# Four short moves in a four-layer graph network: exponentials, a kept product, column sums and copies change their places in the engines' queues

## The chip, the cores and the metric

The kernel runs on one core of a Trainium2 chip. The core has a matrix engine (TensorE, PE in the profile; its weight loads are PEld), VectorE (DVE), ScalarE (ACT), GpSimd (POOL) and SyncE (SP), which here issues the transfers. Each engine works through its own queue in order; an instruction that needs another engine's result waits on a semaphore, and everything behind it in that queue waits too. The metric is device microseconds for one execution; the median over several runs counts. The profile comes from one profiled execution.

## The reference

Input x is 128 batches of 64 nodes with 256 features. Four layers follow each other, each of the form `x = layernorm(x + layer(x))`.

- Layer 0: attention over the graph. `Wh = x W`; scores `leaky_relu(s1[i] + s2[j])`, masked by the adjacency; `softmax(e) Wh`. The softmax is what the change touches.
- Layer 1: attention over 512 edges with four heads, `leaky_relu(Q[src] + K[dst])` against a vector per head, softmax per source node, weighted values, and an output product.
- Layer 2: `A_hat` times x, a product 256 to 512, a batch norm, relu, a product 512 to 256, and a batch norm.
- Layer 3: two graph products (called gcn below), and then for p = 1, 2, 3, 4 an LSTM over windows of p neighbouring nodes; the last hidden state replaces the last node of each window.

```
for p in range(1, MAX_SKIP + 1):
    wins = h[:, :nw * p, :].reshape(Bv * nw, p, Hd)
    last = _lstm_last(Wih[p - 1], Whh[p - 1], bih[p - 1], bhh[p - 1], wins)
    h = h.at[:, idx, :].set(last.reshape(Bv, nw, Hd))
```

## The kernel before

**Layers 0 and 1 (0 to 460 us)** run together. The 8192 rows are cut into 16 chunks (index q) of 512 rows. A main loop over q issues eight steps of layer 1's edge work for chunk q (`l1_graph`: product z in one of two z banks, L357, then ScalarE's relu into u, L359, which sets the bank free). Between these steps the list `between` places pieces of layer 0 for chunks q + 1 and q + 2 and pieces of layer 1's end for an older chunk (`v_a`, `v_b`, `v_c`). `step` makes the scheduler keep each piece's instructions behind the last TensorE instruction of the step before. Layer 0's softmax of a chunk is in `l0_c`: transposed scores, mask, row maximum mx (L271), four exponentials with row sums (L274), and the reciprocal ri (L277). `l0_d` then transposes the exponentials (L283). `l1_qv` makes queries and values of the next chunk: queries m (L320), values m (L323), spad (L332), qs (L330, L331) and, as the last ScalarE instruction of the piece, the values' copy v (L333). L428 reads v on TensorE; L463 and L467 belong to layer 1's sums.

**Layer 2 (524 to 765 us)** computes its 2x2 blocks of products with seven multiplications in place of eight (class `Seven`). `multiply` (L827) fills a bank, `use` (L837 to L855) drains it: product 1 and product 5 are kept (L837; L841 with the bias, on ScalarE), product 3 goes out at L843 or L846, product 6 and 7 are added to kept product 1 on VectorE (L839, L852), and GpSimd adds kept 6 or 7 with 5 into the result (L847, L853). The kept tiles are `kept[0..3]` and one more place in the room of a weight (wq): products 1 alternates between two places by the job's parity, products 5, 6 and 7 have one each. The statistics for the batch norm (L933) go into st1 and st2.

**Layer 3 (765 to 2043 us)** works on four pairs of groups of 16 batches, one `lstm` generator for each pair. Within a pair p = 1 comes first: for groups n = 0, 1 the gates g, i, o as seven products of 512 columns (class `Wide`, TensorE at L1445). These need column sums of the hidden rows, four GpSimd subtractions per group (`column_sums`, L1399 to L1402), written to wx. Then p = 2, 3, 4, with class `Gate` (TensorE at L1708). A gate's products are kept or added on ScalarE (L1723) and VectorE (L1725 to L1736), with GpSimd's two adds in product 7 (L1731, L1732). ScalarE applies the gate's function (L1741), VectorE the products of the cell and the output (L1621, L1622, L1599, L1608), GpSimd the product for gate f (L1618); hidden sums hs follow at L1572 to L1577. The order within each engine is written out by hand: `given` holds each instruction behind the one issued before it on its engine. Helpers record many operations on the line L116.

The `lstm` generator yields at numbered points (units). The table `side` says which other parts advance there: the next pair's gcn with its norm (x2r, L1300; L95, L96, L85, L98, L86, L100), the next weights (`prepare`), and `final` for finished blocks. A block is one of four positions s of a group g. `final` lets GpSimd copy the block out of H into hd (L1843, two copies), turns it (VectorE's stream transpose L1244 into st, a store to way and loads back on SP), adds it to the saved input x3r (L1858), and normalizes and stores it. For the blocks s = 0 to 2 it runs at units u and u + 2, with u = 34 + 4 s + 2 n. The last position reads its values from the tile the LSTM wrote, without copies; the very last two blocks of the kernel are issued after the loop (L1863, L1864).

## Time and profile before

| what | value |
|---|---|
| median of 3 runs | 2041.83 us (2041.1 to 2047.78) |
| the profiled execution | 2044.78 us |
| its span, first to last instruction | 2043.0 us |
| granted TensorE clock, mean | 0.988 |
| TensorE busy | 1938.6 us |
| VectorE busy | 1252.3 us |
| ScalarE busy | 987.1 us |
| GpSimd busy | 878.0 us |

By stage, TensorE is busy 368.8 of the 390 us of layers 0 and 1 behind their start, 231.8 of 241 in layer 2, 353.2 of 365 in pair 0, 305.2 and 305.5 of 310 in pairs 1 and 2, 258.2 of 266 in pair 3, and 13.8 of 27 in the tail.

How to read it: lines of waits give an engine, the line that waited, what it waited for, and then the time in total, the number of times and the longest. Lines of the timeline give the start and the duration in us, the engine, the line, the operation, the tile it writes, the tiles it reads and their shapes, and in brackets the idle time before it and what ended that. Idle time costs something only where the engine that sets the end stands still.

### The profile page before, as it was taken

The page shows a single profiled execution, that of the slowest core. Times are in us where ns is not written, and L with a number is a line of the kernel's source. Part 1 is how long each engine was busy: PE and PEld are TensorE (multiplying, and loading weights), DVE is VectorE, ACT ScalarE, POOL GpSimd, SP SyncE. Part 2 cuts the span into 40 slices and gives each one's busy share as a digit, 9 for nine tenths or more (in the row PEclk, how much of TensorE's full clock was granted, in tenths as well). Part 3 has the DMA queues.
Part 4 walks back from the last instruction along what each step waited for, and adds up shares of the span by engine and source line. Part 5 has one row for each costly group of instructions (what it writes and reads, how often), then busy time and mean ns, then how long its engine had stood idle before and what let it go on. Part 6 is the DMA issues. An engine that isn't in the chain of part 4 may idle for free.

```text
span 2043.0 us, 31508 instructions
## 1 busy us (share of the span) xinstructions
PE 1938.6 (95%) x11447; PEld 1335.4 (65%) x11447; DVE 1252.3 (61%) x2763; ACT 987.1 (48%) x1892; POOL 878.0 (43%) x1017
## 2 busy tenths in 40 slices
PE   5989999998999989899999999999999999999997
PEld 4667777675554446577668477677577667578685
DVE  7465665564456555765566775566865557664566
ACT  2766667766345623644333644343544333543333
POOL 1123333343345543564545544445543435444264
PEclk9999999999899999999999999999999999999999
DMA  6353343332202134432332233132143032131022
GB/s 155 61 73 60 79 79 49 61 56 41 49 22 49 42 123 151 175 125 94 119 140 83 93 130 134 42 130 91 56 152 117 19 114 69 41 119 78 0 64 71
DMA packets 236540, 173.84 MB, mean 85 GB/s; under 512 B 150625, under 2 KB 213601, under 8 KB 233057
## 3 DMA queue, kind: packets, MB, share of 16 engines
q1 hardware_dynamic: 234528, 169.86, 29.3%
q8 instruction: 90, 1.47, 0.3%
q0 software_dynamic: 1024, 1.05, 0.2%
q10 hardware_dynamic: 832, 0.92, 0.1%
q14 instruction: 66, 0.53, 0.1%
HBM read 110.18 MB, written 61.60 MB: 84 GB/s over the span
## 4 chain that ended last, share of the span: by engine, by line
PE 69%; DVE 15%; ACT 5%; POOL 4%; issue 3%; DMA 2%; SPq 1%; DVEq 0%; POOLq 0%; ACTq 0%
PE l L1708 25%; PE l L1664 7%; PE l L1445 4%; PE pz L827 4%; PE pz L756 3%; PE m L253 2%; PE e L348 2%; PE m L320 2%; PE m L442 2%; PE g L1344 2%; PE pz L1025 2%; PE z L357 2%; PE m L323 2%; DVE cell L1622 1%; PE g L1332 1%
## 5 line engine op out<-in xcount | busy, mean ns | idle before, releaser
L1708 PE MATMUL l<-xs,wx 128*128 128x256 f32 (+1 forms) x896 | 277.2, 400 | 5.7 <-DVE gate L1727 3.9
L1708 PE MATMUL l<-hs,wh 128*128 128x256 f32 (+1 forms) x896 | 276.2, 400 | 3.6 <-DVE hs L1572 3.1
L1723 ACT ACTIVATE kept<-l 128x256 f32<-128x256 f32 (+1 forms) x224 | 88.6, 402 | 332.7 <-PE l L1708 331.3
L86 POOL TENSOR_TENSOR ln_rs<-ln_rs,mhalf 128x2 f32<-128x2 f32 (+2 forms) x98 | 86.2, 880 | 358.3 <-DVE ln_rs L98 352.7
L1708 PE MATMUL l<-H,wx 128*128 128x256 f32 (+1 forms) x672 | 210.7, 402 | 4.3 <-DVE gate L1736 3.4
L1708 PE MATMUL l<-hid,wh 128*128 128x256 f32 (+1 forms) x672 | 208.9, 400 | 0.0
L1708 PEld LDWEIGHTS l<-xs,wx 128*128 128x128 f32 x896 | 169.0, 190 | 50.2 <-issue 5.5
L1708 PEld LDWEIGHTS l<-hs,wh 128*128 128x128 f32 x896 | 169.5, 190 | 46.7 <-DVE hs L1572 5.7
L1741 ACT ACTIVATE gate<-gate,bias 128x512 f32<-128x512 f32 (+1 forms) x280 | 170.6, 657 | 42.0 <-DVE gate L1732 34.8
L1664 PE MATMUL l<-H,wx 128*128 128x256 f32 (+5 forms) x672 | 185.2, 432 | 4.9 <-DVE H L116 2.7
L359 ACT ACTIVATE u<-z 128x1024 f32<-128x1024 f32 x128 | 130.3, 1025 | 68.1 <-PE z L357 67.3
L1664 PEld LDWEIGHTS l<-H,wx 128*128 128x128 f32 x672 | 119.0, 190 | 65.3 <-issue 34.1
L1708 PEld LDWEIGHTS l<-H,wx 128*128 128x128 f32 x672 | 125.9, 190 | 42.4 <-DVE gate L1736 7.4
L1708 PEld LDWEIGHTS l<-hid,wh 128*128 128x128 f32 x672 | 127.5, 190 | 31.7 <-issue 2.9
L1731 POOL TENSOR_TENSOR gate<-gate,kept 128x256 f32<-128x256 f32 (+1 forms) x84 | 65.1, 775 | 153.9 <-DVE kept L1729 153.6
L331 DVE TENSOR_TENSOR qs<-m,qs 64x256 fp32r<-64x256 f32 x128 | 53.9, 422 | 105.0 <-ACT qs L330 103.2
L357 PE MATMUL z<-gath_r,qs 128*128 128x512 f32 x256 | 100.2, 479 | 0.7 <-ACT u L359 0.4
L1630 ACT ACTIVATE gate<-cell 128x512 f32<-128x512 f32 (+1 forms) x88 | 58.6, 666 | 85.9 <-DVE cell L1622 63.8
L1576 POOL TENSOR_TENSOR hs<-hid 128x256 f32<-128x256 f32 (+1 forms) x28 | 26.0, 928 | 168.3 <-DVE hid L1608 85.1
L1736 DVE TENSOR_TENSOR gate<-l,gate 128x256 f32<-128x256 f32 (+1 forms) x112 | 50.0, 446 | 61.8 <-POOL gate L1731 37.5
L1618 POOL TENSOR_TENSOR cell<-gate,cell 128x512 f32<-128x512 f32 (+1 forms) x56 | 75.5, 1369 | 28.4 <-ACT gate L1741 28.4
L1725 DVE TENSOR_TENSOR gate<-l,kept 128x256 f32<-128x256 f32 (+1 forms) x112 | 49.1, 439 | 57.1 <-ACT gate L1741 33.0
(375 smaller groups left out, 4090.1 us busy)
## 6 DMA issues: line engine op xcount, KB each, us to landing
wx<-sums SPq DMA_DIRECT2D x9, 2048.0 KB
wh<-sums SPq DMA_DIRECT2D x9, 1792.0 KB
way<-st SPq DMA_DIRECT2D x54, 256.0 KB
st<-way SPq DMA_DIRECT2D x216, 64.0 KB
xin<-in_x SPq DMA_DIRECT2D x16, 512.0 KB
ld<-table SPq DMA_DIRECT2D x16, 512.0 KB
x_dram<-y SPq DMA_DIRECT2D x16, 512.0 KB
x2r<-x_dram SPq DMA_DIRECT2D x32, 256.0 KB
```

Of the source, the lines that this page charges most:

```text
L86: nc.gpsimd.tensor_tensor(dst, dst, mhalf[:, :n], OP.pow)
L357: nc.tensor.matmul(z[:, k, :], L1[q]["qs"][c][:, s, k * P:(k + 1) * P], gath_r, start=True, stop=True)
L359: nc.scalar.activation(u, z, AF.Relu)
L756: nc.tensor.matmul(p_, w1[:, k, m * P:(m + 1) * P], Aq(q)[:, k * QT:(k + 1) * QT], start=k == 0, stop=k == KD - 1)
L827: nc.tensor.matmul(self.bank[at], lhs, rhs, start=first and n == 0, stop=n == len(self.terms) - 1, skip_group_check=True)
L1445: nc.tensor.matmul(self.bank[at], lhs, rhs, start=new, stop=True, skip_group_check=True)
L1618: nc.gpsimd.tensor_tensor(c, t, c, OP.mult)
L1664: nc.tensor.matmul(b, w.raw[0][:, k, at, m, :], x, start=k == 0, stop=k == KD - 1)
L1708: nc.tensor.matmul(self.banks[j], lhs, rhs, start=src == 0, stop=src == 1)
L1723: nc.scalar.activation(self.keep(j), b, AF.Copy)
L1731: e.tensor_tensor(t[0][:, 1], t[0][:, 1], k[5], OP.add)
L1741: given(lambda: nc.scalar.activation(dst, dst, f, bias=b))
```

## The change

It has four parts.

- Layer 0. The four exponentials and the reciprocal become a piece of their own, `l0_x`. In the main loop it is held behind the last ScalarE instruction issued before it (`behind`), which is the values' copy of `l1_qv(q + 1, 0)`, in iterations in which layer 1's own softmax is due (S not negative). In the others it follows `l0_c` as before.
- Layer 2. Kept product 5 alternates between two tiles by the job's parity, kept product 7 has the place in wq. The memory for one more tile comes from st2, which now lies in two pieces in the tiles mask and spads[0].
- Layer 3, p = 1. In pairs 1 to 3 the second group's column sums are issued right behind the first group's, ahead of all gates, and no longer ahead of the first group's gate o. The gcn block with the norms moves from unit 0 (twice) to units 2 and 4 of the pairs 1 and 2.
- Layer 3, `final`. The generator has a further `yield` behind the two copies and is advanced at u - 1, u, u + 2; so the copies are issued one unit before the turn. The yield is in the branch of the blocks 0 to 2.

What the scheduled program shows of it: TensorE's order is the same but for one swap of a values' matmul (L323) with two of L320 in iteration q = 2. On ScalarE the four exponentials move in six places, in the iterations q = 2, 4, ..., 12, from ahead of spad, qs and v to behind v: two of them, a spad, the other two, and then u. On GpSimd the copies L1843 now stand ahead of the add L1731 of gate f (they stood behind it, ahead of L1618), and for the other group ahead of the L1731 of gate i. On SP the block's store to way goes ahead of the first load of x3r. The norms of pairs 1 and 2 go from before the pair's first adds on VectorE to behind the add of product 7, in gate o for the first group and in the second group's gate g for the second.

```diff
@@ l0_c
             mx = small.tile([P, PQ], F32, name="mx")
             nc.vector.tensor_reduce(mx, e, AX.X, OP.max, negate=True)
+            L0[q]["mx"] = mx
+
+        def l0_x(q):
+            e, mx = L0[q]["e"], L0[q]["mx"]
             sm = small.tile([P, PQ], F32, name="sm")
             for c in range(PQ):
                 nc.scalar.activation(e[:, c, :], e[:, c, :], AF.Exp, bias=mx[:, c:c + 1],
...
+        def behind(do, q):
+            if q < NQ:
+                with tc.issue_after([t for t in nc.cur_bb.bb.instructions
+                                     if t.engine == mybir.EngineType.Activation][-1]):
+                    do(q)
+
...
-                [(l1_t, q + 1), (l1_weights, S), (l0_c, q + 2)],
-                [(sums, q), (l1_qv, q + 1, 0)],
+                [(l1_t, q + 1), (l1_weights, S), (l0_c, q + 2)] + [(l0_x, q + 2)] * (S < 0),
+                [(sums, q), (l1_qv, q + 1, 0)] + [(lambda n: behind(l0_x, n), q + 2)] * (S >= 0),
...
-        st2 = wb.tile([P, M2, NQ, 6], F32, name="st2")
+        st2_rooms = [t[:, :NQ * 6].rearrange("p (q s) -> p q s", s=6) for t in (mask, spads[0])]
+
+        class st2:
+
+            def __class_getitem__(cls, at):
+                return st2_rooms[at[1]][(at[0],) + at[2:]]
...
-        kept = [wb.tile([P, QT], F32, name=f"kept{n}") for n in range(4)] + [flat(wq)]
+        kept = [wb.tile([P, QT], F32, name=f"kept{n}") for n in range(5)] + [flat(wq)]
...
-                self.place = {1: kept[n], 6: kept[2], 5: kept[3], 7: kept[4]}
+                self.place = {1: kept[n], 6: kept[2], 5: kept[3 + n], 7: kept[5]}
...
             if n == 0:
                 given(column_sums, 0)
+                if pair:
+                    given(column_sums, 1)
                 yield "begin", 0
             gates = {}
             for name in "gio":
-                if (n, name) == (0, "o"):
+                if (n, name) == (0, "o") and not pair:
                     given(column_sums, 1)
...
@@ final, behind the copies
+            yield
+
...
-                put(k, final(g, s), u, u + 2)
+                put(k, final(g, s), u - 1, u, u + 2)
...
-                    put(k, block, 0, 0)
+                    put(k, block, 2, 4)
```

More of the change, by code (lines that the diff above doesn't have):

```diff
@@ L566 @@
         l0_c(0)
+        l0_x(0)
         l0_a(1)
@@ L574 @@
         l0_c(1)
+        l0_x(1)
         setup_signs()
```

## The prediction

> **What bounds the kernel now.** I read the busy shares first, then the chain that ended last:

> ```profile
> PE 1938.6 (95%) x11447; PEld 1335.4 (65%) x11447; DVE 1252.3 (61%) x2763; ACT 987.1 (48%) x1892; POOL 878.0 (43%) x1017
> ...
> PE 69%; DVE 15%; ACT 5%; POOL 4%; issue 3%; DMA 2%; SPq 1%; DVEq 0%; POOLq 0%; ACTq 0%
> ```

> TensorE is busy 1938.6 of 2043.0 us. The change leaves the matmuls as they are (one pair of small ones swaps places), so it can work only on the 104.4 us in which TensorE stands still. Its own waits come next (us in total, times, longest):

> ```profile
> PE m L428 <- ACT v L333: 9.5, 6, 2.3
> ...
> PE l L1445 <- DVE gate L116: 4.7, 5, 1.1
> ...
> PE l L1708 <- DVE gate L1727: 3.9, 5, 1.0
> ...
> PE l L1708 <- DVE gate L1736: 3.4, 8, 0.4
> PE g L1231 <- DVE st L1229: 3.3, 1, 3.3
> PE m L253 <- issue: 3.1, 1, 3.1
> PE l L1708 <- DVE hs L1572: 3.1, 3, 1.1
> ```

> Each row but L1231 and L253 belongs to a place that the change touches; one more, `PE pz L827 <- ACT kept L841`, is 2.6 us, once. Behind three of the rows stands a wait of VectorE: L1244, the transpose of a finished block, waits for GpSimd's copies at L1843, 41.8 us in 20 waits.

> [...] L1843's copies last 399 ns by the median row and two in a row take 0.74 us, so both readings agree within 10%. [...] under GpSimd's sums two such VectorE adds took 3.17 us, and two multiplies 2.24, where an undisturbed one takes 0.69.

> **A: layer 0's exponentials** (six places; five have a copy of values to gain by). In the timeline ScalarE makes four exponentials (184.53 to 186.17), then spad, qs, and then:

> ```profile
> 186.78 0.60 ACT L333 ACTIVATE v<-m 128x512 f32<-128x512 f32 x1
> 187.28 1.02 ACT L359 ACTIVATE u<-z 128x1024 f32<-128x1024 f32 x1
> ```

> and TensorE, in its timeline:

> ```profile
> 187.43 1.16 PE L428 MATMUL m<-am,v 64*64 64x64 f32 x62 [1.45 <-ACT v L333]
> 188.52 0.73 PE L357 MATMUL z<-gath_r,qs 128*128 128x512 f32 x2
> ```

> With the exponentials behind it, v is ready near 185.0 and the 1.45 us are gone. But TensorE's next work, the z of L357, needs one of two z banks, which the u at 187.28 to 188.29 sets free. ScalarE has no idle time from 184.53 on, and the same instructions (four exponentials of about 0.39, their accumulator reads, spad, qs, v) still stand ahead of that u. It ends at 188.3 to 188.4 again, z starts at 188.45 in place of 188.52: the stall moves one step on, to "z waits for u". Gain 0.07 x 5, say 0.3 in all. Above: if u came in time, 1.45 x 5 = 7.2. Below: the e transposes (L283) and the reciprocal come later; if they came late by 0.2 in each place, +1.0.

> **B: two places for kept product 5, another for 7.** ScalarE's L841 (617.27) waited for GpSimd's L853 (615.98 to 617.24), the last reader of the one place, and TensorE lost 2.55 us at product 3. With two places L841 is done near 613.9. Product 7 then waits for VectorE:

> ```profile
> 617.27 0.69 DVE L933 BATCH_NORM_STATS2 st<-Z 128x6 f32<-128x512 f32 x1 [1.75 <-POOL Z L853]
> 617.88 0.67 DVE L839 TENSOR_TENSOR kept<-pz,kept 128x512 f32<-128x512 f32 x1
> ```

> L839 frees product 7's bank and stands behind statistics that wait for the same L853. It ends at 618.56 as before, against product 7's old start at 618.98: gain about 0.36, between 0 and 2.55. The statistics' rooms in mask and spads[0] add no instruction: 0.

> **C: second group's column sums behind the first's; norms later** (pairs 1 to 3; norms in pairs 1 and 2). Today GpSimd makes the second group's four sums at 1141.42 to 1147.40, and VectorE's SBUF operations queue with them:

> ```profile
> 1146.31 2.24 DVE L116 TENSOR_TENSOR wh<-wh,hs 128x512 f32<-128x512 f32 x2 [0.19 <-ACT wh L116]
> 1148.47 0.68 DVE L116 TENSOR_TENSOR gate<-l,wh 128x512 f32<-128x512 f32 x1
> ```

> TensorE's product 4 waits for that add: 1.12 us at 1148.08, 1459.80 and 1770.96. In the same pair's second group, where no sums run, the multiplies take 0.69 each. Pair 3 has no norms and the same gap, so it is the sums. Moved, they run at about 1132.5 to 1138.5 and end before GpSimd's next duty at 1140.19. The add is there by 1147.2: -1.12 x 3 = -3.4. Against it: in pairs 1 and 2 each norm is 1.95 us of VectorE (L1300 0.69, L95 2x0.37, aggregates 0.30, two small ones 0.22) and 2.3 us of GpSimd (L86, two L100), now ahead of adds that free banks: hid<-l,wh (1150.25, after 1.10 us idle) and cell<-l,wh (1155.34, followed by 0.86 idle), which TensorE needs at about 1157.2 and which would be there at 1157.0 to 1157.8. I take 0.6 per pair back, bounds 0 and 1.15: C = -3.4 + 1.2 = -2.2. The norm's stores on SP move from 1138 to 1158; SP's next load waits for TensorE until 1166.4 and the reader is due at 1174: hidden, with 15 us to spare.

> **D: the finished blocks' copies one unit earlier** (L1843, 24 places of two copies). What they hold up, in pair 0, step 2:

> ```profile
> 1091.28 0.71 DVE L1244 STREAM_TRANSPOSE st<-hd 128x512 f32<-128x512 f32 x1 [0.94 <-POOL hd L1843]
> ...
> 1097.60 0.42 DVE L1727 TENSOR_TENSOR gate<-l,kept 128x256 f32<-128x256 f32 x1
> ```

> From L1244 to L1727 VectorE has no idle time, and TensorE waits 1.02 for L1727 at 1097.15, then 0.43 for L1736. The copies leave GpSimd's queue behind L1731/L1732 (ended 1090.57, copies to 1091.25) and go in front of L1731, where GpSimd is idle 2.77 us. L1244 then starts at 1090.26, 1.02 earlier, and so does all behind it: about 1.0 per pair at step 2, and 0.43 at step 1 (L1244 waits 0.47 there, TensorE 0.43 at 1069.24). 1.43 x 3 pairs = 4.3. Pair 3 has no other filler: TensorE's gaps of 0.49 (1961.33) and 0.79 (1988.94) follow L1244's waits of 3.27 us, and the other final's wait of 0.47 comes twice: 0.49 + 0.79 + 0.94 = 2.2. At its step 3 VectorE waits 0.88 for the block's load; the block's store can leave 1.1 earlier, but ScalarE's L1741 limits the gain to about 0.5. D = -4.3 - 2.7 = -7.0. On SP the block's store (way) now goes out ahead of the first load of x3r, not behind it; both come a unit before their readers, so nothing on the path. Cover of the moved copies: GpSimd's idle time in front of gate f's L1731, 1.09 to 3.24 us, for 0.75 us of copies; the copies queue ahead of L1731, L1732 and then L1618, and VectorE's L1736 and ScalarE wait for those.

> **Sum.** -0.3 - 0.4 - 2.2 - 7.0 = -9.9 us: the profiled execution, 2044.78 with 1.78 outside its span, goes to 2034.9. It stood 2.95 above the median of the runs, 2041.83; with the same difference the median goes to **2032**.

> **Rivals.** (1) *Stalls come back elsewhere.* B gives nothing, C gives back 1.15 per pair (-1.1), and D gains only where VectorE itself was late, about half, -3.5: together -4.6, 2037.2. For it: so many rows with 0.4 us, each with a next wait close behind. Against: L1244's wait is followed by VectorE work without a hole. (2) *All named gaps close.* A -7.2, B -2.55, C -3.4, D -7.1: 2021.6. Against it, the two z banks and L839. (3) *Slower: the copies hold up gate f.* Undisturbed they take 0.75, under VectorE's two-input operations 0.86 each (the longest seen is 867 ns), 1.7 in all, against GpSimd's idle 1.09 in the tightest places. Where they are over 1.1 us, L1731 and after it L1736 and TensorE are late by about 0.6; in all 24 places that is 14.4, and with A to C's -2.9 the time is 2053. It decides from about 1.1 us per two copies in most places; the median of 399 ns speaks against it.

> **How the numbers follow.** My forecast 0.62, its own range 2028 to 2036.5 (C 1.1 and D 2 to either side); rival 1 0.18; rival 2 0.10; rival 3 0.10. 0.3% of the time, 6.1 us, is about what a measurement of this kernel can tell from no change: faster means under 2035.7. That holds for 0.55 of my 0.62, 0.05 of rival 1's 0.18 and all of rival 2: 0.70. Within it: 0.07 + 0.13 = 0.20. Slower: 0.10. The range 2025 to 2040.5 leaves out rival 3 (0.10), most of rival 2 (0.08) and the edge of rival 1 (0.02).

> **What would show it.** A: L428's wait for v shrinks from 9.5 to about 2.3 (the sixth place is untouched), and "z L357 waits for u L359" grows from 0.4 to about 7. B: the wait of L827 for L841 is gone and one of about 2.2 for L839 is there. C: no 1.12 at L1445 in pairs 1 to 3; VectorE's two-input operations there back at 0.69 each. D: L1244's wait for L1843 falls from 41.8 to under 10, and L1708's rows for L1725, L1727, L1736 and L1572 together from 11.7 to about 5. I would be wrong if L1736 waits longer for L1731 than its 37.5 us now, if z meets its bank in time, or if L1445 waits for the moved adds by over 1.1 per pair.

## The result, and the profile after

The changed kernel took 2038.37 us (median, 2034.17 to 2044.66) against 2044.08 for the kernel before in the same comparison: ratio 0.9974, 95% interval 0.9965 to 0.9983, that is 5.3 us faster (3.5 to 7.2). Forecast was a gain of 9.9 us, to 2032. The time lies outside the forecast's own range (2028 to 2036.5) and inside the wide one (2025 to 2040.5); the gain is little more than half. Measured once more on another occasion, on the chip with the number 0, it was 0.9955 (0.9941 to 0.9968), 9.2 us faster. Most of the experiments below are about what lies between these two results. The profiled execution took 2039.12 us, 5.66 less than the one before.

The page of the changed kernel, busy shares and chain:

```profile
PE 1940.1 (95%) x11447; PEld 1337.8 (66%) x11447; DVE 1248.0 (61%) x2763; ACT 988.0 (48%) x1892; POOL 880.0 (43%) x1017
...
PE 73%; DVE 14%; ACT 5%; DMA 3%; issue 3%; POOL 2%; SPq 1%; DVEq 0%; POOLq 0%; ACTq 0%
```

TensorE's idle time fell from 104.4 to 97.2 us, 7.2 us, but it was busy 1.5 us longer for the same matmuls. TensorE's waits of the changed kernel (line numbers are 4 to 22 higher than before: L357 is L361, L428 is L432, L839 is L857, L1244 is L1262, L1727 is L1747, L1736 is L1756, L1858 is L1880):

```profile
PE z L361 <- ACT u L363: 8.9, 6, 1.8
...
PE l L1728 <- DVE gate L1756: 3.4, 8, 0.4
...
PE l L1728 <- DVE hs L1592: 3.1, 3, 1.2
...
PE l L1728 <- DVE gate L1747: 2.7, 4, 1.1
...
PE pz L845 <- DVE kept L857: 2.3, 1, 2.3
...
PE l L1463 <- DVE gate L116: 1.3, 2, 0.8
```

The first and fifth rows are A's and B's stalls in their new places: the 7.2 us at v became waits of z for u, and the 2.55 us at kept product 5 became 2.30 us at product 7, both as forecast. The last row is down from 4.7: C's three gaps are closed. The rows for L1756 and L1592 did not move at all, and L1747 fell only from 3.9 to 2.7: here is D's shortfall. L1244's wait for the copies has left the list of VectorE's waits; two others have come or grown:

```profile
DVE gate L1756 <- POOL gate L1751: 64.3, 42, 3.4
...
DVE x3r L1880 <- DMA st<-way: 2.7, 3, 1.1
```

The first was 37.5 us. It grew by 27 where 41.8 went, but TensorE's row for L1756 is unchanged, so this wait costs nothing. The second was 0.9 us, once, and its growth costs (see D).

The windows view of the changed kernel shows what no line of the waits does. Columns: stretch, its length, busy time of PE, PEld, DVE, ACT and POOL with counts, then the granted clock, the DMA share and GB/s:

```profile
248.00:250.00 2.00, 1.17 (x81) 1.03 (x72) 0.45 (x2) 1.95 (x10) 0.05 (x1) 1.00 0.47 72
250.00:252.00 2.00, 1.04 (x6) 0.80 (x6) 0.07 (x1) 2.00 (x3) 0.90 (x1) 1.00 0.12 28
252.00:254.00 2.00, 1.78 (x6) 1.34 (x5) 0.00 (x0) 2.00 (x4) 0.96 (x1) 0.56 0.00 0
254.00:256.00 2.00, 2.00 (x7) 1.61 (x6) 0.46 (x2) 1.13 (x4) 0.24 (x1) 0.58 0.06 16
```

At 249.17 TensorE waits 1.79 us for u, one of A's moved stalls; shortly behind it the granted clock is one half, from 252.26 to 255.67, for 3.41 us, and the matmuls take about twice as long: four of L324 fill 1.89 us from 252.37 on, and the next four, which begin behind the stretch, at 255.83, fill 0.87. (The expectations below say 3.3 us.) Busy time weighted with one minus the clock, summed over each microsecond of such a stretch, gives 1.6 to 1.7 us lost each time. Over the whole profile it is 16.6 us before and 22.2 after. Of these 5.6 us, 3.5 lie in the first 60 us, where the stretches at half clock fell differently in the two executions: 10.2 us in all before, 17.1 after. Two stretches behind A's stalls add 3.2 and one at 620 us, behind B's, 1.7; around 515 us the profile after lost 2.8 less. That TensorE's busy time grew by only 1.5 us is in part C's doing: its matmuls follow each other more closely (below), by about 2 us in all.

### The profile page after: what moved, and what is told of

It is laid out like the page before. It is cut to its first block, busy times and chain, and to the rows that moved or that the text cites. A ratio compares the mean times of both kernels' runs of the same rounds, so it can differ in the third digit from the quotient of the medians.

```text
span 2037.3 us, 31496 instructions
## 1 busy us (share of the span) xinstructions
PE 1940.1 (95%) x11447; PEld 1337.8 (66%) x11447; DVE 1248.0 (61%) x2763; ACT 988.0 (48%) x1892; POOL 880.0 (43%) x1017
## 4 chain that ended last, share of the span: by engine, by line
PE 73%; DVE 14%; ACT 5%; DMA 3%; issue 3%; POOL 2%; SPq 1%; DVEq 0%; POOLq 0%; ACTq 0%
PE l L1728 27%; PE l L1684 8%; PE pz L845 4%; PE l L1463 4%; PE m L253 3%; PE pz L774 3%; PE m L324 3%; PE e L352 2%; PE m L446 2%; PE g L1362 2%; PE m L327 2%; PE z L361 2%; PE g L1350 2%; PE pz L1043 2%; DVE cell L1642 1%
## 5 line engine op out<-in xcount | busy, mean ns | idle before, releaser
L86 POOL TENSOR_TENSOR ln_rs<-ln_rs,mhalf 128x2 f32<-128x2 f32 (+2 forms) x98 | 85.5, 873 | 367.4 <-DVE ln_rs L98 366.9
L363 ACT ACTIVATE u<-z 128x1024 f32<-128x1024 f32 x128 | 130.3, 1026 | 68.8 <-PE z L361 67.7
L1751 POOL TENSOR_TENSOR gate<-gate,kept 128x256 f32<-128x256 f32 (+1 forms) x84 | 65.1, 775 | 144.9 <-DVE kept L1749 136.2
L335 DVE TENSOR_TENSOR qs<-m,qs 64x256 fp32r<-64x256 f32 x128 | 54.0, 422 | 106.3 <-ACT qs L334 104.4
L361 PE MATMUL z<-gath_r,qs 128*128 128x512 f32 x256 | 100.4, 480 | 9.3 <-ACT u L363 8.9
L1756 DVE TENSOR_TENSOR gate<-l,gate 128x256 f32<-128x256 f32 (+1 forms) x112 | 50.0, 446 | 88.4 <-POOL gate L1751 64.3
```

The source lines that it names most:

```text
L86: nc.gpsimd.tensor_tensor(dst, dst, mhalf[:, :n], OP.pow)
L361: nc.tensor.matmul(z[:, k, :], L1[q]["qs"][c][:, s, k * P:(k + 1) * P], gath_r, start=True, stop=True)
L363: nc.scalar.activation(u, z, AF.Relu)
L1751: e.tensor_tensor(t[0][:, 1], t[0][:, 1], k[5], OP.add)
```

## Experiments

Times are ratios of this kernel to the kernel before in the same comparison, turned into microseconds. Chips differ, so the chip's number stands beside each; the expectations call chip 13 the first, chip 12 the second and chip 0 the third. The clock is the mean over the kernel's timed runs. The ratio is not that of the two medians; the microseconds that it gives differ from the medians' difference by up to 1.8.

| kernel | chip | ratio (95%) | us against before | clock (before's) |
|---|---|---|---|---|
| A alone | 13 | 1.0001 (0.9995 to 1.0008) | +0.2 | 0.9871 (0.9875) |
| B alone | 13 | 1.0014 (1.0008 to 1.0021) | +2.9 | 0.9856 (0.9875) |
| C alone | 13 | 0.9977 (0.9969 to 0.9985) | -4.7 | 0.9877 (0.9875) |
| D alone | 13 | 0.9975 (0.9967 to 0.9983) | -5.1 | 0.9876 (0.9875) |
| A, C, D | 9 | 0.9976 (0.9966 to 0.9986) | -4.9 | 0.9842 (0.9880) |
| changed, exponentials behind u | 9 | 0.9994 (0.9984 to 1.0003) | -1.2 | 0.9829 (0.9880) |
| changed, newer block turned first | 9 | 0.9965 (0.9954 to 0.9976) | -7.2 | 0.9843 (0.9880) |
| C's sums without its norms | 9 | 1.0007 (0.9998 to 1.0017) | +1.4 | 0.9868 (0.9880) |
| A alone | 12 | 1.0028 (1.0016 to 1.0040) | +5.7 | 0.9850 (0.9887) |
| C, D | 12 | 0.9957 (0.9944 to 0.9969) | -8.8 | 0.9876 (0.9887) |
| C, D, newer block turned first | 12 | 0.9946 (0.9934 to 0.9958) | -11.0 | 0.9880 (0.9887) |
| A alone, stall filled | 0 | 0.9999 (0.9990 to 1.0007) | -0.2 | 0.9877 (0.9872) |
| A alone | 0 | 0.9998 (0.9990 to 1.0007) | -0.4 | 0.9874 (0.9872) |
| B alone | 0 | 1.0007 (0.9999 to 1.0016) | +1.4 | 0.9867 (0.9872) |
| changed | 0 | 0.9955 (0.9941 to 0.9968) | -9.2 | 0.9870 (0.9872) |
| A alone | 8 | 0.9994 (0.9985 to 1.0002) | -1.2 | 0.9871 (0.9869) |
| A alone, stall filled | 8 | 0.9998 (0.9989 to 1.0006) | -0.4 | 0.9878 (0.9869) |

### The four parts, each alone

Each of these is the kernel before with one part's hunks of the diff: A has `l0_x` and `behind`, B the five kept tiles with st2's rooms, C the two changes of `column_sums` and the norms' units, D the `yield` in `final` and its unit u - 1. B, for one:

```diff
-        kept = [wb.tile([P, QT], F32, name=f"kept{n}") for n in range(4)] + [flat(wq)]
+        kept = [wb.tile([P, QT], F32, name=f"kept{n}") for n in range(5)] + [flat(wq)]
...
-                self.place = {1: kept[n], 6: kept[2], 5: kept[3], 7: kept[4]}
+                self.place = {1: kept[n], 6: kept[2], 5: kept[3 + n], 7: kept[5]}
```

> Part A alone on the kernel before. Theory (two z banks: the stall moves one instruction on): TensorE's 1.45 us waits of L428 for v go in five places, and waits of z for u of 1.5 to 1.8 us stand there instead; time within 1 us of before, if anything 0.4 to 0.7 us slower. Rival (v's copy was the limit): 5 to 7 us faster.

> Part B alone. Theory (product 7's bank is freed by an add that stands behind statistics which wait for the same GpSimd add): the 2.55 us wait for ScalarE's kept copy turns into one of about 2.3 us for VectorE's kept product 6; time within 0.4 us of before. Rival (the single place was the limit): 2.5 us faster.

> Part C alone. Theory (GpSimd's sums held VectorE's two-input operations): the 1.12 us gap at product 4 of gate o goes in pairs 1 to 3, at most 0.2 us come back in pairs 1 and 2; about 3.0 us faster. Rival (the late norms take part of it back, as forecast): 2.2 us faster or less, with a wait of 0.6 us for an add behind the norms.

> Part D alone. Theory (the copies were the limit only at step 2 of pairs 0 to 2; the 0.43 us behind L1736 is a round trip of TensorE and VectorE, and in pair 3 the add of x3r waits for its block's load, whose store stands on SP behind the output stores of the block before): 0.8 us at step 2 of each of pairs 0 to 2 and 0.3 us in pair 3, 2.8 us faster; VectorE's x3r add waits for the load three times in pair 3, about 2.7 us in all. Rival 1 (the forecast): 7 us faster. Rival 2 (the gain is there but the granted clock takes it back): TensorE's idle time falls by 7 us and its busy time grows by 4.

A was level. B came out at 2.9 us slower where level was expected: the stall moved as foreseen, and in the profile a low clock came behind it. C gained more than either number, D less than the forecast and more than my reading of its gaps. The sum of the four is -6.7 us.

**B.** Timeline of TensorE in the changed kernel, where B's stall ends:

```profile
620.22 1.44 PE L845 MATMUL pz<-seg,SW 128*128 128x512 f32 x2 [2.30 <-DVE kept L857]
621.45 3.30 PE L774 MATMUL pz<-A,w 128*128 128x512 f32 x4
```

And before, where the same four matmuls are on L756:

```profile
618.01 1.13 PE L827 MATMUL pz<-A,SW 128*128 128x512 f32 x2 [2.55 <-ACT kept L841]
618.98 1.02 PE L827 MATMUL pz<-seg,SW 128*128 128x512 f32 x2
619.84 1.88 PE L756 MATMUL pz<-A,w 128*128 128x512 f32 x4
```

They took 1.88 us before and 3.30 after. The windows of the changed kernel there (here for PE alone: stretch, length, busy, granted clock, DMA):

```profile
618.00:620.00 2.00, 0.00 (x0) 1.00 0.93 268
620.00:622.00 2.00, 1.78 (x3) 0.72 1.11 126
622.00:624.00 2.00, 2.00 (x3) 0.50 0.69 5
```

The profiles of all six kernels with B as it stands show this low clock; it begins between 618 and 625 us. Of the thirteen without B, three show one near 617, behind the 2.55 us stall of old; ten, the profile before among them, show none. Matched matmul by matmul, B alone gained 0.3 us by product 7, and had lost 1.5 by 621.98 and behind it. B's cost of 2.9 us on chip 13 was 1.4 on chip 0.

> Part B alone again. Theory (its stall is one instruction later and the clock falls behind it in nearly every execution): 1.3 to 3.5 us slower than before, low clock around 620 us. Rival (chance of the first chip): within 1 us.

On chip 0 the interval reaches to nothing (-0.2 to 3.3), but the profile has the low clock at 619 us again. Together the two say about 2 us, roughly the size of one such stretch (1.7).

> The changed kernel with layer 2's kept places as before (parts A, C and D). Theory (with B, TensorE's idle time before product 7 is followed by 3.3 us at half the granted clock, 1.5 us lost, and without B the idle time before product 3 is not): 1.5 to 3 us faster than the changed kernel, 7 to 8.5 faster than before, and no low clock around 620 us. Rival (the low clock there was chance; B is worth nothing): as the changed kernel, 5.3 faster than before.

Without B the low clock at 620 us is gone, but the time does not tell: A, C and D gained 4.9 us. On this chip the profile had three stretches at half clock behind A's places instead, at 188, 311 and 434 us. This run left B's worth open and pointed to A.

**The stall filled, B.** Product 3 of one job was multiplied twice more:

```diff
...
+                if j == 3 and self.number == 3:
+                    for _ in range(2):
+                        nc.tensor.matmul(self.bank[at], *factor(j, *self.terms[0]), start=False, stop=True,
+                                         skip_group_check=True)
```

> The changed kernel, in which product 3 of the fourth layer 2 job is multiplied three times in place of once (the two repeats, 1.7 us of TensorE's time, fall into the 2.3 us in which TensorE waits for product 7's bank; the block's values are not the reference's). Theory (idle time of TensorE is what lowers the clock): no low clock around 620 us, the eight matmuls behind it at full speed, and product 7 no later than in the changed kernel. Rival (the low clock there has another cause, or the work itself): the clock falls as in the changed kernel.

Both missed. Product 7 came in time with only 0.60 us of idle time and no low clock behind it, but the two repeats held product 3's bank, and TensorE stood still for 3.70 us three microseconds later, with the low clock behind that. So the low clock followed the idle time to its new place; that is in the theory's favour, but the stall was not filled, only moved, and one execution is not a proof.

### A and the clock

A on other chips, alone and with its stall filled. The filled kernel has the hunks of A and this in `v_a`; its two matmuls write what the next ones overwrite:

```diff
             pY = [bank([KD, PQ, N]) for _ in range(2)]
+            if q in (1, 3, 5, 7, 9):
+                for _ in range(2):
+                    nc.tensor.matmul(pY[0].rearrange("p k c n -> p (k c n)"), w0[:, 0, :P], lb,
+                                     start=True, stop=True)
```

> Part A alone once more, beside the next kernels on one chip, for the granted clock. Theory (A's stall, after the small 64 x 64 matmuls, sometimes lets the clock fall to one half, which takes the gain elsewhere back; whether it does depends on the execution): mean granted clock over its runs 0.984 to 0.987, below that of the kernel before by 0.001 to 0.003, and time 0 to 3 us slower. Rival (A has no part in the lower clock): clock and time as before within 0.0005 and 1 us.

> Part A alone on the same chip as the filled one. Theory: 2 to 6 us slower than before, with a mean clock lower by 0.002 to 0.004, as on the second chip; on the first chip the two were level. Rival (the second chip's result was the exception): time and clock as before within 1 us and 0.0007.

> Part A alone a fourth time, beside the filled one. Theory: where the profile shows five waits of z for u of 1.55 to 1.8 us (as on the second chip), three of them are followed by 3.3 us at half the clock and the time is 3 to 6 us above before; where it shows four of about 0.95 (as on the first and third), none is, and the time is that of before. Rival: the clock has nothing to do with the length of these waits.

> Part A alone, and TensorE multiplies twice 128 x 128 x 512 (0.86 us each) into the bank that L432 (L428 before) overwrites right after, in the five places where A leaves it waiting 1.77 us for z's bank; the values stay the same. Theory (the idle time behind the small matmuls is what lets the clock fall): the wait of z for u is under 0.3 us, no low clock behind these places, and the mean granted clock and time are those of the kernel before within 0.001 and 1.5 us, on a chip on which part A alone is slower. Rival (the small matmuls themselves let it fall, idle or not): low clock in two to four of the five places, time as part A alone.

> Part A with TensorE's wait filled, on the same chip. Theory: time as before within 1.5 us and no low clock behind the five places, also where part A alone is 3 to 6 us slower. Rival: as part A alone.

On chip 12 A alone was 5.7 us slower, beyond the 3 us of the theory, at a clock lower by 0.0037; on chips 13, 0 and 8 it was level. Both expectations for chip 0 were misses in that sense; those for chip 8 held. The profiles show where the chips differ. TensorE on chip 12, part A alone, at the third of the five places:

```profile
308.50 1.17 PE L467 MATMUL z<-aht,y 64*64 64x64 f32 x64
309.49 1.12 PE L432 MATMUL m<-am,v 64*64 64x64 f32 x64
312.38 0.73 PE L361 MATMUL z<-gath_r,qs 128*128 128x512 f32 x2 [1.77 <-ACT u L363]
312.95 0.60 PE L287 MATMUL m<-ident,e 128*128 128x128 f32 x4
313.79 1.87 PE L324 MATMUL m<-wq,tT 128*128 128x260 f32 x4 [0.24 <-ACT yT L436]
```

and on chip 0, the same kernel and place:

```profile
305.39 1.12 PE L467 MATMUL z<-aht,y 64*64 64x64 f32 x49
306.90 0.44 PE L467 MATMUL z<-aht,y 64*64 64x64 f32 x12 [0.40 <-issue]
...
309.26 0.73 PE L361 MATMUL z<-gath_r,qs 128*128 128x512 f32 x2 [0.93 <-ACT u L363]
309.83 0.60 PE L287 MATMUL m<-ident,e 128*128 128x128 f32 x4
310.67 1.14 PE L324 MATMUL m<-wq,tT 128*128 128x260 f32 x4 [0.24 <-ACT yT L436]
```

On chip 0 the small 64 x 64 matmuls pause by themselves for 0.4 us and end later, z then waits 0.93 in place of 1.77, and L324 runs at full speed: 1.14 us for four. On chip 12 it takes 1.87. Those pauses are there without A too, in the profiles of B, C and D alone on chip 13. So there are two behaviours: on chips 13, 0 and 8 the pauses are there, z waits under 1 us in four of the five places, and no low clock follows any of them; on chips 9 and 12, and in the profile of the result itself, the pauses are missing, z waits 1.5 to 1.8 us five times, and one to three of these five are followed by half the clock. Three such stretches at 1.7 us are 5 us by estimate, near A's 5.7.

```profile
310.29:313.70 3.41, 1.65 (x81) 1.00 0.05 14
313.70:317.12 3.42, 3.18 (x16) 1.00 0.07 19
371.73:375.14 3.41, 1.66 (x41) 1.00 0.10 26
375.14:378.55 3.41, 3.17 (x8) 0.50 0.03 10
```

The two waits are alike in length, place in the program and busy time of their windows. They differ in where they begin: 1.16 us behind a grid line and 0.51. All 29 waits of z of 1.5 to 1.8 us, over all profiles, divide in this way: the 11 that begin up to 0.54 behind a line, or up to 0.27 ahead of one, are followed by half the clock, and the 18 others are not. Four of these 18 are on chips 13, 0 and 8, where one of the five places keeps its full wait. The old wait for v (1.45 us) was followed by half the clock too, twice in 28, in the profiles of B and of D alone; it began 0.19 and 0.38 behind a line there.

Layer 2 divides as cleanly. Before, the 2.55 us of product 3 lie across a grid line; in the changed kernel the 2.30 us of product 7 lie within one window:

```profile
613.21:616.62 3.41, 2.25 (x5) 1.00 0.51 172
616.62:620.03 3.41, 2.02 (x5) 1.00 1.03 218
```

```profile
617.49:620.90 3.41, 1.11 (x3) 1.00 0.87 234
620.90:624.31 3.41, 3.41 (x6) 0.50 0.84 6
```

In all twenty profiles (for the kernel with B's stall filled the 3.70 us above), where at least 2.04 us of this wait fell into one window of the grid, half the clock followed (ten, all with B among them); where at most 1.96 did, it did not (ten). So B's stall of 2.30 us, shorter than the old 2.55, went with half the clock not by its length, but by where it came to lie. From 140 us on, all 64 full-speed windows of the grid in which TensorE was busy for less than 42% were followed by half the clock, of those between 42% and 56% 33 of 75, of those between 56% and 70% 4 of 205, and of over 10,000 busier ones none. This was read from the profiles afterwards: no run moved a wait along the grid on purpose. Why all six profiles with B had the wait within one window, and what decides between 42% and 70%, stays open.

With the stall filled the waits of z were gone on chips 0 and 8 (one of 0.37 us stayed), no low clock stood behind the five places, and the time was that of before. But part A alone cost nothing on these two, so the filled kernel could not show what it was made for. That A's idle time lowers the clock rests on which waits are followed by it and which are not; it was not shown by taking the idle time away on a chip where A is slow.

**The exponentials behind u.** In the changed kernel the list of step 6 has them, not that of step 5:

```diff
-                [(sums, q), (l1_qv, q + 1, 0)] + [(lambda n: behind(l0_x, n), q + 2)] * (S >= 0),
-                [(v_c, q - LAG - 1), (v_a, q - LAG)],
+                [(sums, q), (l1_qv, q + 1, 0)],
+                [(lambda n: behind(l0_x, n), q + 2)] * (S >= 0) + [(v_c, q - LAG - 1), (v_a, q - LAG)],
```

> The changed kernel, but layer 0's exponentials stand behind the sixth u (L363 there) and not only behind v. Theory (the z bank waits for u, and u stands behind the exponentials on ScalarE): z's wait for u of 1.5 to 1.8 us goes in five places, the transposes of the exponentials wait up to 0.4 us each; about 5 to 6 us faster than the changed kernel, 11 than before. Rival (the stall moves on once more, to the transposes' wait for the exponentials): within 1 us of the changed kernel.

The waits of z for u went in all five places, so u stood behind the exponentials as forecast. But the stall moved on once more, to L324's wait for yT, from 0.24 to 1.21 us, and three places fell to half the clock. It kept 1.2 us of gain over before, not clear of nothing (-3.3 to 0.6), 4 less than the changed kernel in the comparison of the result. Both expectations missed.

### C: what the norms' move is for

Only the column sums move; the norms stay:

```diff
                 given(column_sums, 0)
+                if pair:
+                    given(column_sums, 1)
...
-                if (n, name) == (0, "o"):
+                if (n, name) == (0, "o") and not pair:
```

> Of part C only the column sums, with the norms of pairs 1 and 2 where they were, on the kernel before. Theory (the sums alone free the path; the norms' move only makes room on GpSimd at the pair's start): without the room GpSimd's add wh<-wh (1140.19 before) is late by about 3 us in pairs 1 and 2, TensorE waits there, and only pair 3 gains its 1.8 us: 0 to 2 us faster than before. Rival (the norms' move brings nothing): 5 us faster, as part C whole.

It was 1.4 us slower, with an interval (-0.4 to 3.5) that reaches to nothing; the theory had 0 to 2 us faster, the rival 5. The wait that the theory named is there. GpSimd and TensorE of this kernel in pair 1:

```profile
1142.05 1.09 POOL L100 TENSOR_SCALAR A<-x2r,ln_rs 128x256 f32<-128x256 f32 x2
1143.55 1.26 POOL L116 TENSOR_TENSOR wh<-wh 128x512 f32<-128x512 f32 x1 [0.41 <-DVE wh L116]
```

```profile
1141.48 1.19 PE L1445 MATMUL l<-wx,wh 128*128 128x512 f32 x2 [2.60 <-DVE cell L116]
```

Eight sums in a row end at 1138.8 and the norms, behind them on GpSimd, at 1143.1; VectorE's norms and so its add for the cell are late, and TensorE waits 2.60 us in pair 1 and as much in pair 2. Behind both waits the clock falls to one half, for 3.41 us each, about 3.4 us lost together in this profile, which the theory had not counted. Only pair 3 gains its 1.8 without such a wait. The norms had to leave the pair's start for the sums to have room there.

That the sums were what held VectorE shows in the changed kernel: the two multiplies that took 2.24 us under them read

```profile
1147.59 1.28 DVE L116 TENSOR_TENSOR wh<-wh,hs 128x512 f32<-128x512 f32 x2
```

### D: the store behind the stores

> The changed kernel, but where two finals meet in a unit, the newer block is turned and stored to way before the older block's x3r add, norm and output stores. Theory (in pair 3 the store to way stood on SP behind the older block's output stores): VectorE's waits of the x3r add for the load, 2.7 us in all, go, and TensorE's gaps of 0.82 and 1.08 at L1747 in pair 3 shrink to at most 0.5; 0.8 to 1.5 us faster than the changed kernel. Rival (SP's order does not matter, the load is slow by itself): the waits stay and the time is that of the changed kernel.

```diff
-                u = 34 + 4 * s + 2 * n
-                put(k, final(g, s), u - 1, u, u + 2)
+                f, u = final(g, s), 34 + 4 * s + 2 * n
+                put(k, f, u - 1, u)
+                lates.append((k, f, u + 2))
...
+        for late_part in lates:
+            put(*late_part)
```

SP and VectorE of the changed kernel in pair 3:

```profile
1954.68 1.37 SPq L1890 DMA_DIRECT2D out<-st  x2
1956.15 0.41 SPq L1265 DMA_DIRECT2D way<-st  x1
1956.61 1.28 SPq L1873 DMA_DIRECT2D x3r<-x_dram  x2
1960.28 1.73 SPq L1267 DMA_DIRECT2D st<-way  x4
```

```profile
1952.54 0.70 DVE L1262 STREAM_TRANSPOSE st<-hd 128x512 f32<-128x512 f32 x1
...
1962.11 0.70 DVE L1262 STREAM_TRANSPOSE st<-hd 128x512 f32<-128x512 f32 x1
1963.62 0.69 DVE L1880 TENSOR_TENSOR x3r<-st,x3r 128x512 f32<-128x512 f32 x1 [0.81 <-DMA st<-way]
```

The block is turned by 1953.24, but its store to way goes out at 1956.15, behind the two output stores of the block before, which wait for GpSimd's norm. Its loads follow at 1960.28, and the add that needs them is late by 0.81. With the turn first, the same engines read:

```profile
1948.28 0.34 SPq L1265 DMA_DIRECT2D way<-st  x1
1950.30 1.73 SPq L1267 DMA_DIRECT2D st<-way  x4
1952.13 1.39 SPq L1890 DMA_DIRECT2D out<-st  x2
```

```profile
1947.55 0.70 DVE L1262 STREAM_TRANSPOSE st<-hd 128x512 f32<-128x512 f32 x1
...
1959.90 0.65 DVE L1880 TENSOR_TENSOR x3r<-st,x3r 128x512 f32<-128x512 f32 x1
```

The three waits for the load are gone, and so are TensorE's gaps of 0.82 and 1.08 at L1747 in pair 3; the span from 1750 us to the end of pair 3 is 2.1 us shorter. The time, 7.2 us faster than before, is 2.3 better than A, C and D on the same chip, though it has B as well; the two intervals overlap, so it is the matched 2.1 us that shows the gain.

### C and D without A and B

> Parts C and D without A and B. Theory (A and B bring the lower clock, C and D add up): mean granted clock within 0.001 of before, 9.5 to 10 us faster than before, more than the changed kernel with all four parts by 4. Rival (closing gaps lowers the clock by itself, wherever it is done): 5 to 6 us faster, with a clock lower by 0.0025.

> Parts C and D without A and B, and with the newer block turned first. Theory: the sum of C (4.7), D (5.1) and what the order of the turn brought in pair 3 (about 2), 11 to 12 us faster than before at an unchanged clock. Rival as for C and D: 7 us.

These two are the hunks of C and D alone, the second with the newer block turned first. C and D gained 8.8 us at a clock within 0.0011 of before, near their sum of 9.8; the second gained 11.0, the best of all these kernels (medians of 2030.18 and 2043.01). So C and D carry all of the gain, and A and B carry none.

> The changed kernel beside these. Theory: the sum of C and D (9 us) less what A and B cost on this chip, 3 to 8 us in all, so 1 to 6 us faster than before. Rival (A and B cost nothing when C and D are there): 9 us faster.

The changed kernel itself gained 9.2 us on chip 0, where A is level and B costs about 1.4. The theory's 1 to 6 missed, and 9.2 is the rival's number, though B's low clock is in this profile too. The interval (6.5 to 12.1) also holds C and D's 8.8 less B.

## Why the prediction was right or wrong

**A, "0.07 x 5, say 0.3 in all": right in the mechanism, wrong in what followed.** The stall moved to "z waits for u" exactly where the two z banks put it. The step that failed is the price of the moved stall: I took it as the same time in another place, and left the granted clock out of the sum without a reason. Where the small matmuls did not pause, the wait was 1.5 to 1.8 us in one piece, and where it began up to 0.54 us behind a line of the grid or 0.27 ahead of one, half the clock followed: 5.7 us slower on chip 12, nothing on chips 13, 0 and 8. The bound of +1.0 was far too narrow for that. In the changed kernel's own profile two of the five places are followed by it, 3.2 us.

**B, "gain about 0.36, between 0 and 2.55": wrong in sign.** L857 (L839 before) ends when it did, and product 7 waited 2.30 us for it, as said. The term left out is again the low clock: 1.8 us by the matched profiles (0.3 ahead to 1.5 behind), 2.9 and 1.4 net by the times. The bound from below excluded a loss without a reason.

**C, -2.2: too small by half.** It measured -4.7. The term that was mis-sized is the gap: I counted 1.12 of idle time per pair. Matched matmul by matmul, part C alone gains 0.2 ahead of that gap, 1.3 in it and 0.55 in the matmuls behind it. Before, these followed each other at 0.53 us, not at the 0.43 of part C, without a gap that a view would list: 2.0 per pair. What the late norms give back is 0.4 in each of pairs 1 and 2, against the 0.6 taken.

**D, -7.0: too large.** It measured -5.1, and -4.5 by the matched profiles (two further steps of 0.5 left out; the profile of B alone shows both as well, that of A alone one).
- Step 2 of pairs 0 to 2, "about 1.0 per pair": 0.9 to 1.2. Right.
- Step 1, "0.43 at 1069.24", three times: nothing. All eight waits for L1756 stand at 0.43. Gate o's adds on VectorE from L1747's start to L1756's end take 2.07 us, before (1067.54 to 1069.61) and after (1071.09 to 1073.16), and that is longer than TensorE's products in that stretch (1.70 before). In D alone's profile pairs 0 and 2 gain 0.13 each there and pair 1 loses 0.14. My expectation for D alone called this a round trip between the engines; the timelines show VectorE's own chain.
- Pair 3, "0.49 + 0.79 + 0.94 = 2.2": 0.9 to 1.2 by the matched profiles. The failing words are that the block's store and loads "come a unit before their readers, so nothing on the path". I moved the copies past GpSimd's queue and forgot whom the store then meets on SP. The turn-first kernel gives it back.
- The 0.5 for the block's load at step 3, near the tail: from the matmul at 2016.05 before to TensorE's last end it is 18.17 us, and 18.16 after. Nothing.
- Rival 3, copies that hold up gate f, did not occur: L1756's wait for L1751 grew by 27 us and TensorE's for L1756 by nothing.

**The sum.** C and D together were forecast at -9.2 and gave -8.8: two errors that cancel, which is luck. A and B were forecast at -0.7. Beside C and D, A cost about 4 us (A, C, D: -4.9 on chip 9; C, D: -8.8 on chip 12; the chips differ, so this difference is rough). In the comparison of the result the whole came to -5.3; on chip 0 it came to -9.2, and that this is near the -9.9 is luck of the same kind. Of my signs of error, L1736's longer wait for L1731 came and cost nothing, "z meets its bank in time" and "L1445 waits for the moved adds" did not come; the one that mattered, the granted clock, I had not named. A wait of 1.79 us in layer 1 (at 249.17 in the changed kernel), and 2.04 us of one within one window of the grid in layer 2, were followed by half the clock for 3.41 us. What made chip 13's small matmuls pause and chip 12's not stays open.

## What to carry to other kernels

A stall that moves is not worth zero by that alone: look at what the granted clock does behind it, look whether the profile shows a grid on which the clock changes (3.41 us here), and ask how much of the stall falls between two of its lines. Here a stall of 2.55 us that a line cut in two cost its own length, and one of 2.30 in one window cost 1.7 us more. Because the grid lay differently in each of these profiles, one profile does not tell what such a stall costs; count over several. A part whose gain is nil by its own working is better left out; here the two parts with a real gain did better alone, 8.8 us, than all four (5.3) in the comparison of the result; the chips differ, and on chip 0 all four gave 9.2. When a step is moved forward, follow its data through every queue to the last reader: GpSimd's copy was early, and its block then stood on SP behind another block's stores.

## What the runs showed that I had not expected

- The granted clock fell to 0.50 for 3.41 us behind idle times as short as 1.2 us (L324's with the exponentials behind u), at a cost of 1.6 to 1.7 us each, while the page's mean clock moved only from 0.988 to 0.985. Over the timed runs of one kernel, 0.001 of mean clock went with 0.7 to 1.8 us of time (C and D, with five runs, set aside); in most kernels this is most of the spread between executions.
- The clock changed only on a grid of 3.41 us, and of the 29 waits of z of 1.5 to 1.8 us the 11 that began up to 0.54 us behind one of its lines, or up to 0.27 ahead of one, were followed by half the clock.
- The same program's 64 x 64 matmuls (A alone) ran without a break on chip 12, and with pauses of 0.4 us on chips 13, 0 and 8.
